# One fused two-layer kernel on one Trainium2 core: the copies that empty a side product's PSUM bank are given out at the head of the next turn instead of behind that turn's exponential and maxima

## The chip, the cores and the metric

The kernel runs on one core of one Trainium2 chip, in one launch. The metric is the device time of that launch in microseconds (us); the time of a kernel is the median over its runs.

## What is computed

The input is x, 16 sequences of 512 tokens with 128 features, in float32. Six residual steps follow each other, each on a layer norm of x:

```
x = x + 0.5 * ffn0(layernorm(x))   # 64 channels, 16 relu hinges each, back to 128
x = x + attn0(layernorm(x))        # 16 query heads of 8, 4 key/value heads, rope, causal softmax
x = x + 0.5 * ffn0(layernorm(x))
x = x + 0.5 * ffn1(layernorm(x))   # 8 experts of 128-512-128, each takes its 128 best tokens
x = x + attn1(layernorm(x))        # a gated linear recurrence over the tokens, 64 channels
x = x + 0.5 * ffn1(layernorm(x))
```

The softmax of `attn0` is over 512 keys for each of 16 x 16 x 512 rows, with the row's maximum subtracted; the expert layer routes by softmax and top-k, gathers tokens, runs gelu between two products, and adds the results back.

## The kernel before, in words

**Stages.** The 16 sequences (index b) go through the first layer one behind the other. A main loop (L1073 to L1102) has one pass per sequence. A pass has 44 turns: 4 groups of heads (r) times 11 banks (`BANKS`, L544). In each turn the generator `weights` (L610) issues for sequence b one bank of transposed scores `ps_st` on TensorE (PE; L622), the exponential that reads it into `pt` on ScalarE (ACT; L625) and the causal mask on GpSimd (POOL; L627). In the same turn `maxima` (L550) issues for sequence b + 1 one bank of scores `ps_sc` (L560, L564) and the row maximum that reads it on VectorE (DVE; L569 for one head, L574 for several). After the 16 passes comes the expert layer twice, with the recurrence between: `experts` (L835) is then the main generator, and again one turn follows another.

**Side work.** Everything else is a set of Python generators in two lists, `urgent` and `sides`. `turn()` (L1046) steps each of them once per turn, behind the main work, and so fills the gaps: the norms and their transposes (`norm` L250, `turned` L285: `kan_x`, then `ps_t`, then `kan_xT`), the first feed-forward (`kan` L299: `kan_s`, eight hinges `kan_h` on ACT at L329, products into `ps_kg`, `ps_ko`), the projections and rope of the attention (`attn_in` L375), the splitting of queries and keys into three bf16 parts on ACT and POOL (`parts` L353), the attention's outputs (`outputs` L633: products into `ps_av`, copy to `oT` L651, transposes into `ps_oq` L656, division into `y` L660 and L661), the output projection (`stage_out` L666), routing (L700), gathering and transposing of tokens (`dispatch` L812), and the recurrence (L981).

**Banks.** A side product takes one of two PSUM buffers (`mm`, `bufs=2`, reached through `bank()`, L222); the scores have two buffers each (`scp`, `stp`, L108 and L109), the outputs `ps_av` and the hinge sums `ps_kg` one each. A PE product that takes a buffer again has to wait until the copy that empties it is done, and a product that reads the copy has to wait for it too.

**Order.** Tensor, Scalar, Vector and GpSimd instructions run in the order in which the program issues them (`manual_schedule`, L185); the order of the DMA issues on SyncE (SP) is left to the framework. A side product is issued in one turn, then its generator yields; the instruction that empties its bank is issued when the generator is stepped again in the next turn. By then `weights` and `maxima` of that next turn have been stepped, so on ACT and DVE it stands behind that turn's exponential or maximum. `need` and `take` (L200, L206) keep a budget of work per engine and turn; `need` yields while a turn's budget is spent, `take` only books.

**Where the steps of the prediction lie.** Copies on ACT: `kan_xT`, `yT`, `rope_a`, `rope_b` (all L292), `kan_s` (L307), the emptying of `ps_kg` (L340), `oT` (L651), half of `xin` (L830). On DVE: rope (L387, L393, L401, L407), `va` (L417), `mr` (L599), the division (L660, L661), sums into x (L349, L675, L1023), `scores` (L695), the other half of `xin`, the scan of the recurrence (L1010).

Of the kernel before, what the change touches and what calls it, by code (L numbers as in the profile page):

```python
# [16 lines left out]
P = 128  # L17
# [27 lines left out]
def tile_macaron(  # L45
# [51 lines left out]
    with ExitStack() as ph:  # L97
# [135 lines left out]

        def together(*gs):

            got, live = [None] * len(gs), list(enumerate(gs))
            while live:
                left = []
                for i, g in live:
                    try:  # L240
                        next(g)
                        left.append((i, g))
                    except StopIteration as end:
                        got[i] = end.value
                live = left
                if live:
                    yield
            return got
# [36 lines left out]
        def turned(src, name, pool):  # L285
            ps = yield from bank([P, NT, P], F32, "ps_t", 0.55)
            for c in range(NT):
                nc.tensor.transpose(ps[:, c, :], src[:, c, :], ident)
            yield
            dst = pool.tile([P, S], F32, name=name)  # L290
            take(act=0.6)
            nc.scalar.copy(dst, ps.rearrange("p c q -> p (c q)"))  # L292
            freed()
            yield
            yield from rest(1)
            yield
            return dst

        def kan(b):  # L299

            _, xT = yield from norm(x[b])
            ps = yield from bank([P, S], F32, "ps_s", 0.9)
            nc.tensor.matmul(ps, lhsT=win.rearrange("d a m -> d (a m)"), rhs=xT, start=True, stop=True)
            yield
            sk = w2p.tile([P, S], F32, name="kan_s")
            take(act=0.6)
            nc.scalar.copy(sk, ps)  # L307
            freed()
            yield
            while kan_held[0]:  # L310
                yield
            kan_held[0] = 1

            pg = kap.tile([P, S], F32, name="ps_kg")
            hs = []
            begin = now[0]
            for t in range(HALF + 1):
                while now[0] < begin + 15 * t // 8:
                    yield
                pair = t % 2 == 0 and t > 0  # L320
                work = {"act": 0.8} if t < HALF else {}
                if pair:
                    work["pe"] = 1.0
                if t == 1:
                    work["pool"] = 1.25
                yield from need(**work)
                if t < HALF:
                    h = hp.tile([P, S], F32, name="kan_h")
                    nc.scalar.activation(h, sk, AF.Relu, bias=rbias[:, t : t + 1], scale=kw1[:, t : t + 1])  # L329
                    hs.append(h)  # L330
                if t == 1:
                    nc.gpsimd.tensor_tensor(x[b], x[b], kcst.unsqueeze(1).to_broadcast([P, NT, D]), ALU.add)
                if pair:
                    for i in range(2):
                        nc.tensor.matmul(pg[i * M : (i + 1) * M, :], lhsT=w2d[:, t - 2 + i, :], rhs=hs[t - 2 + i],  # L335
                                         start=(t == 2), stop=(t == HALF))
                yield
            gT = hp.tile([P, S], F32, name="kan_h")
            take(act=0.6)
            nc.scalar.copy(gT, pg)  # L340
            kan_held[0] = 0
            kans[0] -= 1
            yield
            po = yield from bank([P, NT, D], F32, "ps_ko", 0.9)
            for c in range(NT):
                nc.tensor.matmul(po[:, c, :], lhsT=gT[:, bass.ts(c, P)], rhs=wout, start=True, stop=True)
            yield
            take(dve=0.7)
            nc.vector.tensor_add(x[b], po, x[b])  # L349
            freed()  # L350
            yield
# [23 lines left out]
        def attn_in(b, st):  # L375
# [8 lines left out]
            nc.tensor.matmul(pa, lhsT=wq.rearrange("k h d -> k (h d)"), rhs=xT, start=True, stop=True)  # L384
            yield
            take(dve=0.7)
            nc.vector.tensor_mul(ta, pa, rope[:, 0, :])  # L387
            freed()
            pb = yield from bank([P, S], F32, "ps_pb", 0.9)
            nc.tensor.matmul(pb, lhsT=wqr.rearrange("k h d -> k (h d)"), rhs=xT, start=True, stop=True)  # L390
            yield
            take(dve=0.7)
            nc.vector.tensor_mul(tb, pb, rope[:, 1, :])  # L393
            freed()
            pk = yield from bank([2 * KR, S], F32, "ps_pk", 0.9)
            nc.tensor.matmul(pk, lhsT=wk.rearrange("k w h d -> k (w h d)"), rhs=xT, start=True, stop=True)
            yield
# [3 lines left out]
            nc.vector.tensor_mul(ka, pk[0:KR, :], rope[0:KR, 0, :])  # L401
            pv = yield from bank([P, NT, KR], F32, "ps_v", 0.9)
            for c in range(NT):
                nc.tensor.matmul(pv[:, c, :], lhsT=xT[:, bass.ts(c, P)], rhs=wv, start=True, stop=True)
            yield
            take(dve=0.7)
            nc.vector.tensor_mul(kb, pk[KR : 2 * KR, :], rope[KR : 2 * KR, 1, :])  # L407
# [3 lines left out]
            yield  # L411

            take(dve=0.3)
# [3 lines left out]
            nc.vector.tensor_copy(va[:, :, :, 0:HD], pv.rearrange("p c (r d) -> p c r d", d=HD))  # L417
# [160 lines left out]
        def max_rows(b, half, maxs):  # L578
# [15 lines left out]
            for c in range(NT):  # L594
                nc.tensor.transpose(pm[:, c, :], ms[:, c, :, :].rearrange("p i h -> p (i h)"), identb)
            yield
            mr = w2p.tile([3 * H2, S], BF16, name="mr")
            take(dve=0.4)
            nc.vector.tensor_copy(mr, pm.rearrange("p c q -> p (c q)"))  # L599
# [33 lines left out]
        def outputs(b, st, r):  # L633
# [4 lines left out]
            for c in range(NT):  # L638
                if c == 1:
                    yield  # L640
                if c < 2:
                    yield from need(pe=1.0 if c == 0 else 1.4)
                n = S - c * P
                for g in range(NG):
                    nc.tensor.matmul(po[32 * g : 32 * g + 32, c * P : S], lhsT=va[:, c, r, :],  # L645
                                     rhs=pt[:, g, OFF[c] : OFF[c] + n], start=(c == 0), stop=(c == NT - 1))
                if c in (0, NT - 1):
                    yield
            oT = w2p.tile([P, NT, P], F32, name="oT")
            yield from need(act=0.6)  # L650
            nc.scalar.copy(oT.rearrange("p c q -> p (c q)"), po)  # L651
# [3 lines left out]
            for c in range(NT):  # L655
                nc.tensor.transpose(pq[:, c, :, :].rearrange("p r w -> p (r w)"), oT[:, c, :], ident)  # L656
            yield
            rd = small.tile([P, NT, NG, 1], F32, name="rden")
            take(dve=0.55)
            nc.vector.reciprocal(rd, pq[:, :, :, HD : HD + 1])  # L660
            nc.vector.tensor_mul(y[:, :, r, :, :], pq[:, :, :, 0:HD], rd.to_broadcast([P, NT, NG, HD]))  # L661
# [4 lines left out]
        def stage_out(b, st):  # L666
# [4 lines left out]
            for c in range(NT):  # L671
                nc.tensor.matmul(po[:, c, :], lhsT=yT[:, bass.ts(c, P)], rhs=wo, start=True, stop=True)
            yield
            take(dve=0.7)
            nc.vector.tensor_add(x[b], po, x[b])  # L675
# [10 lines left out]
        def gated(k, b):  # L686
# [4 lines left out]
            for c in range(NT):  # L691
                nc.tensor.matmul(ps[:, c, :], lhsT=xT[:, bass.ts(c, P)], rhs=gateT, start=True, stop=True)
            yield
            take(dve=0.2)
            nc.vector.tensor_copy(scores[b // GB][:, :, b % GB, :], ps)  # L695
# [116 lines left out]
        def dispatch():  # L812
            while taken[0] < NR * B:
                yield
            for i in range(0, len(order), 2):
# [10 lines left out]
                for j in range(2):  # L826
                    nc.tensor.transpose(ps[:, j, :], xgs[i // E % 2][:, i % E + j, :], ident)
                yield
                copy = nc.vector.tensor_copy if i % 4 else nc.scalar.copy
                copy(xins[i // E % 2][:, i % E : i % E + 2, :], ps)  # L830
# [150 lines left out]
        def recurrence(pair):  # L981
# [6 lines left out]
            for a in range(2):  # L988
                nc.tensor.matmul(pf[half[a], :], lhsT=wf, rhs=xTs[a], start=True, stop=True)
            yield  # L990
            fg = w2p.tile([P, S], F32, name="fg", tag="kan_s")
            nc.scalar.activation(fg, pf, AF.Tanh, scale=0.5)
# [5 lines left out]
            nc.tensor.matmul(pl, lhsT=wlam, rhs=fg, start=True, stop=True)  # L998
            yield
            lam = w2p.tile([P, S], F32, name="lam", tag="oT")  # L1000
            nc.scalar.activation(lam, pl, AF.Tanh, bias=lbias, scale=0.25)
# [4 lines left out]
            for a in range(2):  # L1006
                nc.tensor.matmul(pu[half[a], :], lhsT=wb, rhs=xTs[a], start=True, stop=True)
            yield
            s = w2p.tile([P, S], F32, name="s", tag="y")
            nc.vector.tensor_tensor_scan(s, lam, pu, 0.0, ALU.mult, ALU.add)  # L1010
# [3 lines left out]
            def leave(a, b):  # L1014
                po = yield from bank([P, NT, D], F32, "ps_h2")
                for c in range(NT):
# [3 lines left out]
                    if c == 1:  # L1020
                        yield
                yield
                nc.vector.tensor_add(x[b], po, x[b])  # L1023
# [22 lines left out]
        def turn():  # L1046
            urgent[:] = [g for g in urgent if step(g)]
# [13 lines left out]
        for _ in range(8):  # L1061
            step(first)
# [10 lines left out]
        for b in range(-1, B):  # L1073
# [12 lines left out]
            for i in range(TURNS):  # L1086
                step(wts)
# [8 lines left out]
                turn()  # L1096
            step(mxs)
# [10 lines left out]
        while step(main) or sides:  # L1108
# [56 lines left out]
```

## Time and profile before

| what | value |
|---|---|
| median of 3 runs | 1751.41 us (1749.4 to 1756.8) |
| the profiled execution's own time | 1746.91 us |
| its span | 1745.2 us, 35245 instructions |
| PE busy | 1636.9 us (94%) |
| PE weight loads busy | 1111.0 us (64%) |
| DVE busy | 1107.3 us (63%) |
| ACT busy | 996.6 us (57%) |
| POOL busy | 977.6 us (56%) |
| mean granted PE clock | 0.971 |

The profile is of one execution. A line of groups gives the source line, the engine, the operation, what is written and read, the number of instructions, their busy time, the mean duration of one in ns, and the idle time of the engine just before them with what ended it. The start and end of a matmul are partly modelled: a row may say 0.38 us where the next matmul starts 0.22 us later. Busy PE is therefore not PE at its peak, and start-to-start times say more. `PEld` is the loading of the stationary operand, which overlaps the products.

### The profile page before, as it was taken

The numbers are of one execution on the slowest core, as the hardware profiler recorded it, in microseconds if no ns is written. First come the engines' busy times: TensorE is split into PE (matmuls) and PEld (weight loads), VectorE is DVE, ScalarE is ACT, GpSimd is POOL, SyncE is SP. The second block draws the span as 40 slices with busy tenths as digits, with TensorE's granted clock in tenths as the row PEclk, the third lists the DMA queues.
The fourth block names the chain that finished last, engine by engine and source line by source line (L and its number), as shares of the span: only waits on it lengthen the run. The fifth ranks groups of instructions, "written<-read, shape, count | busy, mean of one in ns | idle before, by whom it ended". The sixth has DMA issues, their size and how long they took to land. (4 is left out here: it accounts for less than half of the span.)

```text
span 1745.2 us, 35245 instructions
## 1 busy us (share of the span) xinstructions
PE 1636.9 (94%) x12879; PEld 1111.0 (64%) x12879; DVE 1107.3 (63%) x3604; ACT 996.6 (57%) x2000; POOL 977.6 (56%) x1453
## 2 busy tenths in 40 slices
PE   6788999999999999899899899999999999999997
PEld 2334444444444444444444389899988889989997
DVE  6677767777787788788876137643467444672222
ACT  3445667777777776677667654344443334444443
POOL 2524535545565455455534767567663777647773
PEclk9889999999999999999999899999998999999999
DMA  4211111011110111011122113233322233323342
GB/s 117 76 52 36 44 44 43 28 42 51 54 37 32 42 55 47 16 48 54 35 70 63 31 44 73 51 64 73 62 60 45 55 73 63 66 56 71 68 82 48
DMA packets 101753, 94.77 MB, mean 54 GB/s; under 512 B 11859, under 2 KB 90140, under 8 KB 101340
## 3 DMA queue, kind: packets, MB, share of 16 engines
q1 hardware_dynamic: 74512, 67.45, 12.5%
q0 software_dynamic: 26048, 24.93, 8.8%
q8 instruction: 101, 1.65, 0.4%
q14 instruction: 72, 0.59, 0.1%
q10 hardware_dynamic: 1020, 0.15, 0.0%
HBM read 58.93 MB, written 37.49 MB: 55 GB/s over the span
## 5 line engine op out<-in xcount | busy, mean ns | idle before, releaser
L625 ACT ACTIVATE pt<-ps_st 128x512 f32<-128x512 f32 (+1 forms) x704 | 386.9, 561 | 238.3 <-PE ps_st L622 232.9
L627 POOL TENSOR_SCALAR_AFFINE_SELECT pt<-pt 128x128 f32<-128x128 f32 (+2 forms) x704 | 247.0, 355 | 405.0 <-ACT pt L625 400.4
L569 DVE CUSTOM_DVE_ANT_0 below<-ps_sc,causal 128x512 bf16<-128x512 f32 (+1 forms) x512 | 316.5, 618 | 117.2 <-PE ps_sc L564 103.1
L881 ACT ACTIVATE mo<-ps_h 128x512 f32<-128x512 f32 x256 | 153.1, 598 | 262.2 <-PE ps_h L879 262.0
L805 POOL DMA_INDIRECT xg<-xnd,tokI x256 | 249.9, 976 | 80.5 <-issue 42.8
L879 PE MATMUL ps_h<-xin,mw 128*128 128x128 f32 x2048 | 281.1, 281 | 0.0
L894 PE MATMUL ps_y<-mw,mo 128*128 128x128 f32 x2048 | 274.7, 278 | 0.0
L564 PE MATMUL ps_sc<-kp,qp 72*128 72x512 bf16 (+3 forms) x1024 | 260.7, 307 | 10.6 <-DVE maxs L569 8.0
L622 PE MATMUL ps_st<-qp,kp 99*128 99x512 bf16 (+3 forms) x1024 | 259.8, 307 | 5.7 <-ACT pt L625 4.8
L879 PEld LDWEIGHTS ps_h<-xin,mw 128*128 128x128 f32 x2048 | 252.7, 194 | 6.3 <-issue 3.7
L926 POOL DMA_INDIRECT sum<-ye,tokI x124 | 201.3, 1624 | 97.7 <-ACT ye L897 31.2
L894 PEld LDWEIGHTS ps_y<-mw,mo 128*128 128x128 f32 x2048 | 251.7, 194 | 2.3 <-issue 1.0
L622 PEld LDWEIGHTS <-kp 99*128 99x128 bf16 x1024 | 94.2, 101 | 203.8 <-issue 185.4
L329 ACT ACTIVATE kan_h<-kan_s,rbias,kw 128x512 f32<-128x512 f32 x256 | 206.6, 814 | 7.1 <-PE ps_kg L335 6.9
L574 DVE TENSOR_REDUCE maxs<-ps_sc 128x2 f32<-128x512 f32 (+1 forms) x192 | 130.6, 685 | 70.5 <-PE ps_sc L564 69.3
L335 PE MATMUL ps_kg<-kan_h,w2d 128*64 128x512 f32 x512 | 164.7, 640 | 3.1 <-ACT kan_h L329 3.0
L645 PE MATMUL ps_av<-pt,va 128*32 128x512 f32 (+3 forms) x2048 | 166.8, 444 | 0.0
L564 PEld LDWEIGHTS <-qp 72*128 72x128 bf16 x1024 | 97.5, 100 | 55.6 <-issue 33.9
L900 DVE TENSOR_TENSOR mo<-mo 128x128 bf16<-128x128 f32 x132 | 38.3, 290 | 137.8 <-ACT mo L885 137.6
L912 PE MATMUL acc<-mo 128*128 128x128 bf16 x1584 | 113.0, 220 | 6.0 <-DVE mo L900 5.8
L912 PEld LDWEIGHTS <-mo 128*128 128x128 bf16 x1584 | 99.5, 99 | 23.8 <-issue 22.5
L645 PEld LDWEIGHTS ps_av<-pt,va 128*32 128x32 f32 x2048 | 53.6, 109 | 93.0 <-issue 49.7
(195 smaller groups left out, 2308.8 us busy)
## 6 DMA issues: line engine op xcount, KB each, us to landing
qp<-qs SPq DMA_DIRECT2D x64, 288.0 KB
xnd<-kan_x SPq DMA_DIRECT2D x32, 256.0 KB
sum<-x SPq DMA_DIRECT2D x31, 256.0 KB
qs<-qpart SPq DMA_DIRECT2D x48, 128.0 KB
kp<-ks SPq DMA_DIRECT2D x48, 96.0 KB
x<-in_L_attn_x_dram SPq DMA_DIRECT2D x16, 256.0 KB
mw<-in_L_ffn_w_dram SPq DMA_DIRECT2D x16, 256.0 KB
xg<-xnd,tokI POOLq DMA_INDIRECT x256, 2.5
```

The lines of the kernel that those rows point to most:

```text
L329: nc.scalar.activation(h, sk, AF.Relu, bias=rbias[:, t : t + 1], scale=kw1[:, t : t + 1])
L564: nc.tensor.matmul(v[:, u, 0:n], lhsT=qp[r][0 : 9 * HD, g, bass.ts(c, P)], rhs=kp[0 : 9 * HD, r, 0:n], start=alone, stop=(u == len(gs) - 1 ...
L569: nc.vector.tensor_tensor_reduce(below[:, 0:n], v[:, 0, 0:n], causal[:, S - n : S], 1.0, LOWEST, ALU.add, ALU.max, accum_out=maxs[:, c, h ...
L622: nc.tensor.matmul(v[:, u, 0:n], lhsT=kp[ROWS, r, bass.ts(c, P)], rhs=qp[r][ROWS, g, c * P : S], start=True, stop=True)
L625: nc.scalar.activation(o, v[:, :, 0:n], AF.Exp, scale=HD ** -0.5)
L627: nc.gpsimd.affine_select(out=dg, in_=dg, compare_op=ALU.is_ge, fill=0.0, base=0, pattern=[[0, len(gs)], [1, P]], channel_multiplier=-1)
L645: nc.tensor.matmul(po[32 * g : 32 * g + 32, c * P : S], lhsT=va[:, c, r, :], rhs=pt[:, g, OFF[c] : OFF[c] + n], start=(c == 0), stop=(c == ...
L805: nc.gpsimd.indirect_dma_start(out=xgs[i // E % 2][:, i % E, :], out_offset=None, in_=xnd[b], in_offset=bass.IndirectOffsetOnAxis(ap=tokI[ ...
L879: nc.tensor.matmul(pst[:, f, :], lhsT=mw1[e][:, bass.ts(f, P)], rhs=xins[i // E % 2][:, i % E, :], start=True, stop=True)
L894: nc.tensor.matmul(py, lhsT=hs[u][:, f, :], rhs=mw2[e][:, f, :], start=(f == 0), stop=(f == NF - 1))
L912: nc.tensor.matmul(acc[:, c, :], lhsT=sels[u][:, bass.ts(c, P)], rhs=yes[u][:, w, :], start=(e == 0 and c == 0 and w == 0), stop=(e == las ...
L926: nc.gpsimd.indirect_dma_start(out=sums[k, b], out_offset=bass.IndirectOffsetOnAxis(ap=tokI[g][:, n : n + 1], axis=0), in_=ye[:, b % 2 * ( ...
```

## The change

A list `later` and a function `flush()` are added. Where a side product has been issued, the instruction that empties its bank is no longer issued after the generator's next step but put into `later` at once, before the yield. `flush()` stands at the head of every turn, ahead of `weights` and `maxima` (ahead of `experts` in the second part), and issues what has gathered. So on ACT and DVE these instructions stand ahead of the exponential or maximum of the turn, not behind it. What is booked with `take`, and when a bank counts as free for the next product, stays in its place. In `outputs` the copy of `ps_av` to `oT` had waited for budget (`need`); it now only books (`take`). The two memsets of `va` on POOL are issued a turn earlier, with the product `ps_v`. Left in place are the set-up code, the routing's own copies (L729, L755 to L757) and everything that reads no side product (the hinges L329, the parts L356 and L362, the statistics).

The core of the diff; each of the other places has the same form as one of these:

```diff
+        later = []
+
+        def flush():
+            for emit in later:
+                emit()
+            later.clear()
+
...
             for c in range(NT):
                 nc.tensor.transpose(ps[:, c, :], src[:, c, :], ident)
-            yield
             dst = pool.tile([P, S], F32, name=name)
+            later.append(lambda: nc.scalar.copy(dst, ps.rearrange("p c q -> p (c q)")))
+            yield
             take(act=0.6)
-            nc.scalar.copy(dst, ps.rearrange("p c q -> p (c q)"))
             freed()
...
+                if c == NT - 1:
+                    oT = w2p.tile([P, NT, P], F32, name="oT")
+                    later.append(lambda: nc.scalar.copy(oT.rearrange("p c q -> p (c q)"), po))
                 if c in (0, NT - 1):
                     yield
-            oT = w2p.tile([P, NT, P], F32, name="oT")
-            yield from need(act=0.6)
-            nc.scalar.copy(oT.rearrange("p c q -> p (c q)"), po)
+            take(act=0.6)
...
-            yield
             rd = small.tile([P, NT, NG, 1], F32, name="rden")
+
+            def divide():
+                nc.vector.reciprocal(rd, pq[:, :, :, HD : HD + 1])
+                nc.vector.tensor_mul(y[:, :, r, :, :], pq[:, :, :, 0:HD], rd.to_broadcast([P, NT, NG, HD]))
+
+            later.append(divide)
+            yield
             take(dve=0.55)
-            nc.vector.reciprocal(rd, pq[:, :, :, HD : HD + 1])
-            nc.vector.tensor_mul(y[:, :, r, :, :], pq[:, :, :, 0:HD], rd.to_broadcast([P, NT, NG, HD]))
             freed()
...
         def turn():
+            flush()
             urgent[:] = [g for g in urgent if step(g)]
             sides[:] = [g for g in sides if step(g)]
             refill()
...
             for i in range(TURNS):
+                flush()
                 step(wts)
                 step(mxs)
...
-        while step(main) or sides:
+        working = True
+        while working or sides:
+            flush()
+            working = step(main)
             turn()
```

The same is done to `kan` (`kan_s`, the emptying of `ps_kg`, the sum into x), to `attn_in` (four rope products, `va`), to `max_rows` (`mr`), to `stage_out`, `gated`, `dispatch`, `recurrence` and `leave`.

In the built program the order on PE is the same instruction for instruction. Of 2009 instructions on ACT, 291 stand ahead of at least one that they stood behind; of 3476 on DVE, 364; on POOL the 26 memsets of `va`; and on SP, where the framework orders, some 20 of 445 issues stand one to three places elsewhere.

## The prediction, made blind

> **What bounds the kernel now.** I read the page's busy shares first, then busy time by stretch, then PE's waits within stretches, then the order of time around one wait.
>
> ```profile
> PE 1636.9 (94%) x12879; PEld 1111.0 (64%) x12879; DVE 1107.3 (63%) x3604; ACT 996.6 (57%) x2000; POOL 977.6 (56%) x1453
> ```
>
> PE sets the time; no other engine exceeds 64%. By stretch (width, then busy time of PE, PEld, DVE, ACT, POOL, then PE clock, DMA share, GB/s):
>
> ```profile
> 0.00:150.00 150.00, 113.80 (x498) 48.30 (x502) 102.56 (x295) 67.19 (x109) 54.30 (x96) 0.87 0.24 75
> 150.00:250.00 100.00, 90.56 (x639) 44.66 (x635) 72.17 (x232) 61.95 (x118) 50.17 (x104) 0.93 0.14 45
> 250.00:650.00 400.00, 393.78 (x2836) 193.46 (x2837) 310.41 (x1026) 301.90 (x555) 213.47 (x443) 1.00 0.13 43
> 650.00:955.00 305.00, 282.77 (x2045) 138.07 (x2044) 247.12 (x801) 209.05 (x387) 145.68 (x317) 0.98 0.15 47
> ...
> 1300.00:1400.00 100.00, 93.07 (x724) 80.33 (x724) 67.42 (x227) 34.12 (x83) 55.44 (x54) 0.92 0.24 50
> ```
>
> The steady passes (250 to 650) leave PE 6.2 us idle in 400; 650 to 955, where routing joins DVE, 22.2 in 305. Only PE's idle time is to be had, and only what an emptying ends. PE's waits in 250 to 650 are these two (total, times, longest):
>
> ```profile
> PE ps_s L303 <- ACT kan_xT L292: 5.0, 7, 0.7
> PE ps_o L672 <- ACT yT L292: 1.1, 7, 0.2
> ```
>
> and in 650 to 955 the largest are
>
> ```profile
> PE ps_t L288 <- DVE y L661: 6.7, 4, 2.9
> PE ps_ko L346 <- DVE rope_kb L407: 2.1, 1, 2.1
> PE ps_sc L564 <- DVE maxs L574: 1.7, 4, 0.7
> PE ps_sc L564 <- DVE maxs L569: 1.5, 4, 0.5
> PE ps_m L595 <- DVE rope_kb L407: 1.3, 2, 0.7
> ```
>
> All but the two `maxs` rows end on an emptying that the change moves. How one arises (start, duration):
>
> ```profile
> 507.02 0.33 PE L622 MATMUL ps_st<-qp,kp 99*128 99x384 bf16 x1
> 507.14 0.52 ACT L625 ACTIVATE pt<-ps_st 128x384 f32<-128x384 f32 x1
> 508.08 0.62 ACT L362 CAST kpart<-rope_ka 32x512 bf16<-32x512 f32 x1 [0.42 <-POOL rope_ka L359]
> 508.61 0.57 ACT L292 COPY kan_xT<-ps_t 128x512 f32<-128x512 f32 x1
> 509.08 0.95 ACT L625 ACTIVATE pt<-ps_st 128x384 f32<-128x384 f32 x2
> 509.23 1.12 PE L303 MATMUL ps_s<-kan_xT,win 128*128 128x512 f32 x2 [0.71 <-ACT kan_xT L292]
> ```
>
> The transposes behind this copy ended at 506.86. The copy ran 1.75 us later, behind the turn's exponential and a cast that waited for POOL; PE stood until it ended. The same stall repeats in each pass.
>
> [...] the copy above had its input and still waited for its queue; a 0.38 us score product is followed 0.22 us later by the next. So a PE wait of w on the page is w + 0.16 from start to start, and I add 0.16 us per wait removed. [...] Here some waits are for the bank (`ps_t` for `y`), others for the data (`ps_s` for `kan_xT`); both end with the same copy. [...] after the 2.9 us wait that ended at 909.4, the clock in 909 to 913 is 0.57.
>
> **The change, part by part.** The order on PE is the same, instruction for instruction; ACT, DVE and POOL execute the same instructions. Only the time at which banks and copies, exponentials and maxima are ready can move.
>
> *Removed: waits for emptyings.* An emptying moves ahead of one exponential (0.46 to 0.60 us), or one reduction (0.55 to 0.69), and of the casts or statistics between, and of their own waits. I credit the smaller of the wait and the distance moved.
> 250 to 650: 6.1 us in 14 waits, each of at most 0.7 against 1.1 or more moved: 6.1 + 14 x 0.16 = 8.3.
> 650 to 955: `y` four times 0.65 = 2.6 of its 6.7 (the rest is DVE's backlog ahead of it); `rope_kb` 1.1 of the one long wait and 1.3 of the two short; `va` 1.5, `kan_xT` 1.1, `mr` 0.7, `rope_a` and `rope_b` 1.2, `kan_h` of L340 0.3; with 0.16 for ten or so removed whole, 11.5.
> 150 to 250: of `rope_kb` 2.3, `y` 2.7 and `kan_xT` 0.6, about 5.8 with the 0.16s. 955 to 1050: 2.2 (mostly `oT`). Expert part: `xin` 2.7 and the scan 1.9, of which about 3.7. Before 150: 0.9.
> Sum of credits: 32.4 us.
>
> *Added: exponentials and maxima are later.* Behind an emptying now wait its turn's exponential, and behind that the hinges, casts and POOL's mask. PE waits for the exponential when it takes the same `ps_st` two banks on. I measured this spare time for every bank: start of its first L622 minus end of the exponential two banks before. In 250 to 650 the smallest is 0.145 us, a tenth lie under 0.25, the median is 1.29; 0.05 of each is the signal (509.18 to 509.23 above). Each moved emptying makes its exponential later by its own duration, 0.57 to 0.60, less what ACT idled there; what exceeds the spare time is a new stall. Over the 94 moves in 250 to 650 that is 8.7 us in 28 turns (mostly `oT` and `kan_xT`, in the short turns in the middle of a head group); 3.3 in 650 to 955, 1.5, 0.7 and 1.0 in the other three: 15.2. The same for maxima: 3.6, nearly all before 150 and in 650 to 955. Together 18.8 if nothing absorbs them. In the expert part the gelu and the scaled copies have more spare time than a copy takes; cost zero, up to 2 if not.
>
> *How the two meet.* I walked the stretch 506 to 514 by hand. `oT` ahead puts the exponential of 506.3 back to 506.9 and the L622 of 507.02 to 507.38; `kan_xT` ahead (now 507.3) puts the next L622 from 507.80 to 508.35; L303 starts at 508.9, not 509.23; then two copies stand ahead of the exponential of 511.05, and the L622 of 511.85 is no earlier than before; L672 starts 0.3 earlier. Stalls of 1.19 leave, delays of 1.11 arrive, 0.35 remains. So in the steady passes the credit nearly cancels: seven times 0.35, less 0.2 a pass for delays elsewhere in it, is 1.0. Elsewhere credit less cost is 11.5 - 4.5 = 7.0, 5.8 - 0.7 = 5.1, 2.2 - 1.5 = 0.7, 3.7 in the expert part, and 0.9 - 2.8 = -1.9 at the start. Total 15.6. In the routing stretch DVE has a backlog of two to three instructions when PE waits, so what is next late is often another DVE result; I keep about 70%: **11 us**.
>
> *Moved at no cost.* The memsets of `va` (0.42 and 0.13 us) go ahead of one mask; the mask's readers, the `ps_av` products, come turns later; without that cover 0.55 a pass, 8 us. `take` for `need` in `outputs` changes no budget that matters, since PE's order is unchanged. SP: some 20 issues shift one to three places of about 0.7 us (a part of the keys goes behind the row maxima's transfer); kp and qp are for a later pass; PE's stalls ending on a DMA there are two, 2.9 us, so I bound it by 0 and 3 and take 0. `mr` comes earlier, and its DMA with it.
>
> Base: 1746.9 (profiled execution; span 1745.2) - 11 = 1735.9. Runs stand at 1751.41 / 1746.91 = 1.0026 of it: **1740 us**.
>
> **Rivals.**
> *No change.* Credit is passed on everywhere as in the steady pass (30% of 32.4 = 9.7) and half the costs arrive (9.4): 1751. For it: the walk. Against: outside the steady passes few moved exponentials are short of spare time.
> *Slower: late exponentials.* The costs arrive in full (18.8) and reach the hinges: four `ps_kg` products at 466.80 take 1.64 us and at 481.20 1.95, against 1.01, because they wait for a hinge that stands behind an exponential; a further 0.33 at two places in 16 passes is 10.5. With half the credit (16.2): 29.3 - 16.2 = +13, 1764. It decides once the delays not absorbed exceed the credit kept. Against it: an emptying's input is complete on PE before the turn's scores are, so it never holds ACT for PE longer than the exponential did.
> *Clock.* From the clocks by stretch, half-rate time after 150 is about 60 us (14, 12, 13, 5, 16), some 30 us of loss, each begun by a wait of 2 us or more. If shorter waits spare a third of it, 10 more: 1730. It can also go the other way by a few us[...].
> *Not done as said*: excluded by the order on ACT and DVE.
>
> **Chances.** Forecast 0.52 (its own range 1732 to 1749), no change 0.21, slower 0.13, clock 0.14. Low 1728 leaves about half of the clock case out, high 1756 the slower one; with the tails about 0.2. A measurement can tell 0.5%, 8.8 us, from no change. Faster by more, under 1742.6: two thirds of the forecast and the clock case, 0.48. Slower, over 1760.2: most of that rival, 0.12. Same: 0.40.
>
> **What would show it.** `kan_xT`, `yT` and `oT` start within 0.7 us of their products' end; PE's waits for `kan_xT` at L303 vanish; the waits for `y` drop by about 0.6 each; PE's waits for `pt` at L622 grow by several us. The forecast is wrong if those grow by more than the others shrink, if `ps_kg` pairs lengthen, or if half-rate stretches come or go.

## The result, and the profile after

| | before | after |
|---|---|---|
| median | 1751.39 us (1749.4 to 1756.8, 4 runs) | 1731.26 us (1727.0 to 1734.0, 4 runs) |
| the profiled execution, its span | 1746.9, 1745.2 | 1733.8, 1732.0 |
| its mean granted PE clock | 0.971 | 0.972 |

The ratio is 0.9885, 95% interval [0.9869, 0.9901]: 20.1 us faster by the medians, 13.1 by the two profiled executions. The traces can explain the 13.1 only. Two other runs of the changed kernel took 1727.0 and 1728.7 us at a mean clock of 0.980 and 0.979, so part of the rest is clock that differs from run to run. (The trace's record of the PE clock has two values, 1.0 and 0.5; a half-rate stretch below is a time at 0.5.)

The changed kernel's page, busy shares:

```profile
PE 1629.2 (94%) x12879; PEld 1112.0 (64%) x12879; DVE 1119.1 (65%) x3604; ACT 1001.4 (58%) x2000; POOL 980.0 (57%) x1453
```

PE has 7.7 us less for the same products (the clock has a part in it, see below). DVE has 11.8 us more, with the same 3604 instructions. By stretch, in the columns shown for the kernel before:

```profile
0.00:150.00 150.00, 112.37 (x492) 48.31 (x493) 101.94 (x293) 67.11 (x108) 54.32 (x95) 0.85 0.24 75
150.00:250.00 100.00, 94.07 (x649) 46.35 (x648) 73.76 (x241) 64.60 (x120) 50.93 (x107) 0.91 0.14 47
250.00:650.00 400.00, 392.91 (x2824) 194.62 (x2824) 321.54 (x1017) 299.56 (x551) 213.19 (x440) 1.00 0.13 43
650.00:955.00 305.00, 285.60 (x2129) 141.84 (x2127) 248.57 (x815) 219.76 (x405) 156.29 (x334) 1.00 0.15 49
...
1300.00:1400.00 100.00, 94.45 (x764) 84.31 (x763) 59.14 (x209) 34.73 (x83) 56.15 (x54) 0.91 0.28 56
```

The steady stretch does 12 products fewer than before in the same 400 us, with 11.1 us more on DVE. From 650 to 955 PE does 84 more, at a clock of 1.00 (before 0.98). PE's waits from 250 to 650, then from 650 to 955:

```profile
PE ps_sc L574 <- DVE maxs L584: 3.4, 7, 0.5
PE ps_sc L574 <- DVE maxs L579: 3.4, 14, 0.4
```

```profile
PE ps_t L297 <- DVE y L672: 5.0, 4, 1.9
PE ps_st L632 <- ACT pt L635: 4.1, 10, 0.7
PE ps_kg L344 <- ACT kan_h L338: 2.0, 2, 1.0
PE ps_sc L570 <- DVE maxs L579: 1.8, 4, 0.6
...
PE ps_ko L356 <- DVE rope_kb L415: 0.8, 1, 0.8
```

In the steady stretch the waits for `kan_xT` and `yT` are gone, and 6.8 us of waits for maxima stand in their place. From 650 to 955 the waits for `y` and `rope_kb` have shrunk.

**Where the time went.** PE's order is the same in all kernels of this study, so I compare when PE begins the first score product (L622 before, L632 after) of each pass. After less before, summed up: +0.6 us at pass 1, -1.6 at pass 3, +0.7 at pass 9, -13.1 at pass 15, -14.1 at the first expert product, -13.1 at the end. A steady pass (the median of passes 4 to 8) takes 55.57 us before and 55.97 after: it has become longer. All of the gain lies in passes 1 to 2 and 9 to 15.

**What holds the steady pass.** The groups of DVE in 250 to 650 that make `kan_x`, in the changed kernel:

```profile
L283 DVE TENSOR_SCALAR kan_x<-x,ln_mv,ln_rstd 128x128 f32<-128x128 f32 x28 | 21.3, 801 | 0.0
L287 DVE TENSOR_TENSOR kan_x<-x,ln_rstd 128x512 f32<-128x512 f32 x21 | 15.6, 742 | 0.0
```

and in the kernel before:

```profile
L278 DVE TENSOR_TENSOR kan_x<-x,ln_rstd 128x512 f32<-128x512 f32 x21 | 15.6, 742 | 0.0
L274 DVE TENSOR_SCALAR kan_x<-x,ln_mv,ln_rstd 128x128 f32<-128x128 f32 x28 | 10.5, 419 | 0.0
```

The same 28 instructions (L274, now L283; they normalise x ahead of the router, four per pass) take 801 ns in place of 419: 10.8 us more, in a window in which DVE grew by 11.1 in all (per whole pass, 1.5 of 1.9). The timeline of the changed kernel shows how (start, duration; "x2" and "x3" are instructions in a row):

```profile
506.94 0.56 ACT L299 COPY kan_xT<-ps_t 128x512 f32<-128x512 f32 x1
508.48 1.02 PE L312 MATMUL ps_s<-kan_xT,win 128*128 128x512 f32 x2
...
511.06 1.35 POOL L637 TENSOR_SCALAR_AFFINE_SELECT pt<-pt 128x256 f32<-128x256 f32 x3
511.14 1.61 DVE L283 TENSOR_SCALAR kan_x<-x,ln_mv,ln_rstd 128x128 f32<-128x128 f32 x2
...
512.67 0.68 DVE L584 TENSOR_REDUCE maxs<-ps_sc 128x4 f32<-128x512 f32 x1
...
513.12 1.27 POOL L341 TENSOR_TENSOR x<-x,kcst 128x512 f32<-128x512 f32 x1
513.27 1.46 DVE L283 TENSOR_SCALAR kan_x<-x,ln_mv,ln_rstd 128x128 f32<-128x128 f32 x2
...
513.40 0.38 PE L574 MATMUL ps_sc<-kp,qp 72*128 72x512 bf16 x1 [0.53 <-DVE maxs L584]
```

`kan_xT` starts early and its product has no wait, as meant. But the first `kan_x` of 511.14 starts just after POOL's masks have started, takes 1.35 us by its own record, and is done 0.08 us after the last of the three; the second of the pair takes 0.34. The next pair falls on POOL's addition of 1.27 us and takes 1.20 + 0.33. In the kernel before the two pairs stand like this:

```profile
511.99 0.59 DVE L274 TENSOR_SCALAR kan_x<-x,ln_mv,ln_rstd 128x128 f32<-128x128 f32 x2
513.10 0.91 DVE L274 TENSOR_SCALAR kan_x<-x,ln_mv,ln_rstd 128x128 f32<-128x128 f32 x2
```

Three of these four took 0.34 us, one 0.66. The maximum behind is late by what is lost, and PE waits for its bank. The profile shows DVE as busy in this, not idle (0.0 in the rows above): only the duration of the instruction tells.

What these traces show is this: beside POOL's work the instruction takes 1.35 and 1.20 us where 0.33 is usual, and both times it ends 0.08 us after that work. The first of these lasted over three short masks in a row, not one instruction. How the two engines hold each other up no trace shows; below it is called the collision.

### The profile page after: what moved, and what is told of

It reads as the page before. It is cut to its first block, busy times and chain, and to the rows that moved or that the text cites. A ratio compares the mean times of both kernels' runs of the same rounds, so it can differ in the third digit from the quotient of the medians.

```text
span 1732.0 us, 35235 instructions
## 1 busy us (share of the span) xinstructions
PE 1629.2 (94%) x12879; PEld 1112.0 (64%) x12879; DVE 1119.1 (65%) x3604; ACT 1001.4 (58%) x2000; POOL 980.0 (57%) x1453
## 5 line engine op out<-in xcount | busy, mean ns | idle before, releaser
L635 ACT ACTIVATE pt<-ps_st 128x512 f32<-128x512 f32 (+1 forms) x704 | 379.6, 560 | 130.9 <-PE ps_st L632 127.9
L632 PE MATMUL ps_st<-qp,kp 99*128 99x512 bf16 (+3 forms) x1024 | 258.7, 305 | 9.9 <-ACT pt L635 9.2
L632 PEld LDWEIGHTS <-kp 99*128 99x128 bf16 x1024 | 93.5, 100 | 204.6 <-issue 186.8
```

The source lines that it names most:

```text
L632: nc.tensor.matmul(v[:, u, 0:n], lhsT=kp[ROWS, r, bass.ts(c, P)], rhs=qp[r][ROWS, g, c * P : S], start=True, stop=True)
L635: nc.scalar.activation(o, v[:, :, 0:n], AF.Exp, scale=HD ** -0.5)
```

## Experiments

Each kernel was timed beside the kernel before on its own chip, and ratios are to that. Five chips were used in all; the kernel before took 1785.5 us on that of e1 to e4, 1832.7 with e5 to e8, 1746.8 with e9 to e11 and 1748.4 with e12. In the first eight runs the expert part, here all that follows the last bank of scores, took 785 to 834 us (750 on the first chip), for reasons that I did not settle, so their ratios say little of the passes, and I read these from traces: there the chips agree (the changed kernel's steady pass is 55.97 and 55.99 us on two of them). "Pass" is the steady pass (median). "Up to 9" is what has been lost or won against the profile before when pass 9 begins, "9 to 16" what is lost or won from there to the last bank of scores of pass 15, in us.

| run | early | normalisation `kan_x` | ratio, interval | pass | up to 9 | 9 to 16 |
|---|---|---|---|---|---|---|
| before | none | as before | 1 | 55.57 | | |
| after | all | as before | 0.9885 [0.9869, 0.9901] | 55.97 | +0.7 | -14.9 |
| e1 | ScalarE's | as before | 1.0045 [1.0022, 1.0068] | 56.64 | +3.7 | -0.3 |
| e2 | VectorE's | as before | 0.9898 [0.9870, 0.9927] | 55.59 | -3.6 | -12.7 |
| e3 | ScalarE's; VectorE's from pass 9 | as before | 0.9955 [0.9938, 0.9973] | 56.64 | +8.0 | -8.1 |
| e4 | all | summing form | 0.9879 [0.9851, 0.9908] | 54.49 | -12.3 | -15.7 |
| e5 | all | as before | 0.9801 [0.9761, 0.9840] | 55.99 | +0.1 | -13.9 |
| e6 | none | summing form | 1.0000 [0.9972, 1.0027] | 56.24 | +5.7 | +3.8 |
| e7 | ScalarE's | summing form | 0.9965 [0.9942, 0.9987] | 55.42 | +1.4 | +1.6 |
| e8 | all | summing form, two steps | 1.0001 [0.9976, 1.0025] | 55.79 | -0.4 | +4.3 |
| e9 | none | as before | 1.0042 [1.0028, 1.0057] | 56.24 | +3.2 | -0.4 |
| e10 | all | on ScalarE | 0.9936 [0.9923, 0.9949] | 55.13 | -4.0 | -14.2 |
| e11 | the division | as before | 0.9986 [0.9977, 0.9995] | 55.61 | -1.2 | +0.6 |
| e12 | all | on ScalarE in the passes | 0.9906 [0.9889, 0.9922] | 55.67 | -1.7 | -14.6 |

In e1 to e11 the two memsets of `va` stand where the change puts them. So the order to hold e1, e2, e6, e7 and e11 against in the passes is that of e9, which has the memsets alone (56.24), not that of the kernel before. One rule says what is given out early; the rest is issued behind its `take`, as before:

```diff
+        def give(engine, emit):
+            if early(engine):
+                later.append(emit)
+                return lambda: None
+            return emit
...
-            later.append(lambda: nc.scalar.copy(sk, ps))
+            put = give("act", lambda: nc.scalar.copy(sk, ps))
             yield
             take(act=0.6)
+            put()
```

**One half of the change each.** My first theory was that the copies moved on ScalarE win in the steady passes and the operations moved on VectorE lose there. e1 has `early` true for "act", e2 for "dve", e3 for "act" and, from pass 9 on, for "dve" too.

> Only the emptyings on ScalarE stand ahead of the exponential; those on VectorE stand behind the maxima as before. Theory D (the gain comes from VectorE's emptyings in the passes with routing, the loss in the steady passes from maxima that now come late): a steady pass takes 55.0 us instead of 55.6 before and 56.0 changed, passes 10 to 15 gain only 3 of the 14 us, in all 8 us faster (0.995). Rival A (the gain is ScalarE's, whose copies are the ones that PE waited for in every pass): nearly the whole 20 us stays (0.989), passes 10 to 15 included.

> Only the emptyings on VectorE stand ahead of the maxima; those on ScalarE stand behind the exponential as before. Theory D: a steady pass takes 56.0 us or more, passes 10 to 15 gain 9 us or more, in all 8 to 10 us faster (0.995). Rival A: steady pass as before, 55.6, passes 10 to 15 gain at most 4, in all 4 us or less (0.998).

> ScalarE's emptyings go ahead everywhere, VectorE's only from pass 9 on, where routing begins to load VectorE. Theory D: a steady pass takes 55.0 us, passes 10 to 15 gain what the full change gains, in all 5 to 6 us faster than the full change, 24 us faster than before (0.986). Rival A: no different from the full change (0.989). If the passes before 3 need VectorE's emptyings, 2 to 3 us of it are lost.

The theory fell. ScalarE's half alone makes the pass longer (56.64 us) and the kernel slower; VectorE's half alone leaves the pass at the length that it has in the kernel before, 0.65 us below e9, and brings nearly all of the gain (in the passes 16.3 us, where the whole change brings 14.2). e3 had been meant as a better version and wins less than half as much. The `kan_x` of e1 that normalises ahead of the router (L283 in the changed kernel), in 250 to 650:

```profile
L294 DVE TENSOR_SCALAR kan_x<-x,ln_mv,ln_rstd 128x128 f32<-128x128 f32 x28 | 19.4, 734 | 0.0
```

and both kinds in e2:

```profile
L298 DVE TENSOR_TENSOR kan_x<-x,ln_rstd 128x512 f32<-128x512 f32 x21 | 20.8, 990 | 0.0
L294 DVE TENSOR_SCALAR kan_x<-x,ln_mv,ln_rstd 128x128 f32<-128x128 f32 x28 | 11.5, 451 | 0.0
```

In e1 the `kan_x` ahead of the router takes 734 ns where e9, without ScalarE's half, has 418. I take it that this half shifts exponentials, and so masks, onto it. In e2 it is the other kind that has grown, by 5.2 us in the stretch; DVE is busy 2.0 us more per pass than before, and yet the pass is no longer. What this costs and what the early operations save come out even there; I did not separate them.

**The collision taken away.** That the form of the normalisation that also sums would not be held up was an assumption of mine; e4 is the whole change with it:

```diff
                     nc.vector.tensor_scalar(xl[:, c, :], xt[:, c, :], mv[:, c, 0:1], rstd[:, c : c + 1],
-                                            ALU.subtract, ALU.mult)
+                                            ALU.subtract, ALU.mult, accum_out=unused[:, c : c + 1])
```

In this form the kernel leaves out the multiplication by the inverse deviation (so in e6 and e7 too). The router and the experts then work on other values, so of these three only the passes are read.

> The full change, but the normalization that writes kan_x (TENSOR_SCALAR, 128x128, the one whose mean went from 0.42 to 0.80 us in the steady passes) also writes out an unused accumulator. Theory P (it got slower because it now falls onto GpSimd's masks[...]): its duration in the steady passes is the same everywhere, under 0.5 us with the accumulator's read, a steady pass is back at 55.5 us or below, 3 us faster than the full change (0.987). Rival M (maxima are late simply because an emptying stands ahead of each): the pass stays at 56.0 and the time at 0.989 or a little more.

The pass falls to 54.49 us, the shortest of all; from pass 3 to 9 the trace lists no wait of PE at all. The form's mean is 398 ns here, 400 in e6 and 399 in e7: one duration in three orders. Its groups in e4, in 250 to 650:

```profile
L295 DVE TENSOR_SCALAR_CACHE_REDUCE kan_x<-x,ln_mv,ln_rstd 128x128 f32<-128x128 f32 x28 | 10.1, 398 | 0.0
L295 DVE DVE_READ_ACCUMULATOR kan_x<-x,ln_mv,ln_rstd 128x1 f32 x28 | 2.3, 81 | 0.0
```

**Form or collision?** The next four ran on one chip. e5 is the change itself again. e6 and e7 put the form of e4 into the order before and into e1. e8 is the whole change in two operations of that form, the second multiplying, with nothing left out:

```diff
-                    nc.vector.tensor_scalar(xl[:, c, :], xt[:, c, :], mv[:, c, 0:1], rstd[:, c : c + 1],
-                                            ALU.subtract, ALU.mult)
+                    nc.vector.tensor_scalar(xl[:, c, :], xt[:, c, :], mv[:, c, 0:1], None,
+                                            ALU.subtract, ALU.add, accum_out=unused[:, c : c + 1])
+                    nc.vector.tensor_scalar(xl[:, c, :], xl[:, c, :], rstd[:, c : c + 1], None,
+                                            ALU.mult, ALU.add, accum_out=unused[:, c : c + 1])
```

> The whole change once more, on the chip that ran the half changes, whose own kernel before takes 1785.5 us. If the two halves simply add: the exponential half alone was 1.0045 and the VectorE half alone 0.9898, so 0.9942. If the VectorE half does in the whole change what it does alone, and the ScalarE half costs nothing beside it: 0.990. The first chip showed 0.9885. Steady pass: 56.0 us as on the first chip (before 55.6).

> The order of the kernel before, with only the four normalising subtractions per pass in the form that also sums (the multiplication by the inverse deviation is left out there, and stays out of the output). If the collision of this operation with GpSimd's masks is something that the change brought about, little is to be had here: kan_x falls from 419 ns to about 320 ns with its sum, four per pass, beside PE's work: 0 to 0.3 us a pass, ratio 0.997 to 1.000. If the form itself is what gave the earlier full change without the collision its 1.1 us a pass, it gives the same here: steady pass 54.4, ratio about 0.989.

> Only ScalarE's emptyings early, and the normalising subtraction in the form that sums (the multiplication by the inverse deviation is left out). If ScalarE's half lengthens the steady pass through the collision (56.6 us against 55.6), the pass falls under that of the kernel before, to 54.5 to 55.3, and the ratio to 0.985 to 0.995. If it lengthens it through the exponentials and copies behind which other ScalarE work waits, the pass stays at 56.3 to 56.6 and the ratio at 1.003.

> The whole change, with the normalisation in two operations of the form that sums, one subtracting and one multiplying, so that the output is the reference's. VectorE has some 0.64 us for each of the four instead of 0.80 as the collision left them, in about 2.6 us per pass and without variation. If the collision is what lengthens the pass, it is 54.5 to 55.0 us and the ratio 0.982 to 0.989, better than the change as it is. If VectorE's busy time is what counts, the pass stays at 56 us and the ratio at that of the whole change.

e5 repeats the passes of the change, 13.8 us by the last; its ratio is lower than this gives, which must come from outside the passes; the kernel before has no profile on that chip, and it stays open. In e6 the form wins nothing over e9, which has the same order (both 56.24), so the form is not a gain in itself. In e7 ScalarE's half, which had lengthened the pass, lies below the kernel before (55.42) and 0.82 below e6: the lengthening was the collision, not late exponentials. e8 shows no collision (means of 340 and 347 ns in 250 to 650), but its two operations keep DVE busy for 0.66 us per normalisation, not much less than the collision had (0.76), and its pass is again near that of the change. So it is DVE's time at this place that counts, whether the collision or a longer form takes it.

Pairs of runs that differ only in this normalisation say how much. From pass 3 to 9, with time in which two records overlap counted once, the pass grows by 1.48 us for 1.62 more of `kan_x` per pass (after against e4), 1.22 for 1.20 (e1, e7), 1.30 for 1.24 (e8, e4), and not at all for none (e6, e9): about one for one. DVE is busy 80% of the steady stretch and yet paces it, through the maxima queued on it. This holds within one order, not across orders, as e2 shows, and only as long as the maxima are what PE waits for: e10, without this work on DVE, stays 0.64 above e4, with PE waiting for `pt`.

That e8 lost all gain from pass 9 to 16 I had not expected. Its half-rate time there is 34 us, against 3 to 7 in e4, e5 and the change. Half of PE's busy time in such a stretch, where the recorded clock is 0.5, is an estimate of what it costs (a stretch of 10.2 us in e3, below, cost 4.6): 16.3 us in e8, 3.1 in e5, so 13 of the 18 us between them.

**The memsets, the engine, and the division.** e9 has the order before on PE, ACT and DVE, and only the memsets moved. e10 takes the normalisation to ScalarE:

```diff
+                nc.gpsimd.tensor_tensor(shift, mv[:, :, 0], rstd, ALU.mult)
+                nc.gpsimd.tensor_scalar(shift, shift, -1.0, None, ALU.mult)
...
-                    nc.vector.tensor_scalar(xl[:, c, :], xt[:, c, :], mv[:, c, 0:1], rstd[:, c : c + 1],
-                                            ALU.subtract, ALU.mult)
+                    nc.scalar.activation(xl[:, c, :], xt[:, c, :], AF.Identity, bias=shift[:, c : c + 1],
+                                         scale=rstd[:, c : c + 1])
```

e11 has only `divide` early (L671, L672).

> The order of the kernel before on PE, VectorE, ScalarE and SyncE; of the change only what it moves on GpSimd's queue and in the code, the two memsets of va, is left in. I had put this at nothing. Passes within 0.3 us of those of the kernel before in sum, ratio 0.998 to 1.002. If the memsets' place matters, some of the gain before pass 9 is here.

> The whole change, with the normalisation of one kind of pass moved to ScalarE as four activations with scale and bias (GpSimd works out the bias in two small operations), [...] the output stays the reference's. If what lengthens the steady pass and the passes 10 to 15 is VectorE's maxima coming late, by the collision or by its busy time: steady pass 54.2 to 54.9 us (56.0 with the change), passes 9 to 16 at least 15 us shorter in all than before, ratio 0.972 to 0.985, better than the whole change by 8 to 13 us. If ScalarE has no room for four more operations of about 0.3 us a pass, the pass stays above 55.5.

> Only the two operations that make y out of a turned product (a reciprocal and a multiplication, 16 pairs per pass) are given out ahead; all other emptyings are where they were before. VectorE's half alone won 12.7 us in passes 9 to 16, 3.6 before pass 9. If PE's waits for y are what that was, nearly all of the 12.7 is here: 10 to 13 us, ratio 0.990 to 0.994. If the gain is from the rotary products, va and the additions to x, it is below 4 us.

e9 missed: the memsets that I had put at nothing lengthen the pass by 0.67 us and the kernel by 0.4%. They fill a time in which POOL stood idle (0.97 us ahead of the mask at 501.42 in the kernel before), and its additions behind them come 0.5 to 0.8 us earlier in the pass. The first of these now meets a small cast on DVE, which takes 1.02 us there in place of 0.26. The next meets the other `kan_x`, a product of two SBUF operands, which the cast has made 0.7 us later. Each happens once per pass. The casts of e9 in 250 to 650, then those of the kernel before:

```profile
L619 DVE CAST ms<-ms_r 128x32 bf16<-128x32 f32 x15 | 8.6, 570 | 0.0
```

```profile
L589 DVE CAST ms<-ms_r 128x32 bf16<-128x32 f32 x15 | 3.2, 214 | 0.0
```

The product in e9's timeline, and its group in 250 to 650 (742 ns before):

```profile
505.04 1.25 POOL L453 TENSOR_TENSOR rope_ka<-rope_ka,rope_kb 32x512 f32<-32x512 f32 x1
...
505.64 1.29 DVE L298 TENSOR_TENSOR kan_x<-x,ln_rstd 128x512 f32<-128x512 f32 x1
...
506.26 0.82 POOL L658 TENSOR_SCALAR_AFFINE_SELECT pt<-pt 128x128 f32<-128x128 f32 x1
```

```profile
L298 DVE TENSOR_TENSOR kan_x<-x,ln_rstd 128x512 f32<-128x512 f32 x21 | 19.0, 906 | 0.0
```

The product ends 0.64 us after the addition, about its time alone (0.68), and the mask that starts at 506.26 takes 0.82 us where one of its size takes 0.29 with nothing beside it (0.75 beside this product in the kernel before): as if each stood for the other in turn. Cast and product together take 1.25 us more per pass, of which 0.67 reach its length. e2, e6 and e11, which share the memsets' place, show both (casts of 572 to 626 ns).

e10 shortened the pass to 55.13, less than expected (PE's waits in it are now for `pt`, 2.5 us in six passes), and its expert part took 758.1 us in place of 750.6: there ScalarE's activation of `kan_x` stands among the gelus (from 980 to 1560, 136 of 482 ns each, where the changed kernel has 136 of 360 ns on DVE).

e11 missed too. The division alone gives all that VectorE's half gave in the steady pass (55.61, against 56.24 in e9), but nothing in passes 9 to 16. What differs there between e11 and e2 is therefore the rest of that half. PE's waits in passes 9 to 15, in e11:

```profile
PE ps_t L308 <- DVE y L694: 5.2, 4, 2.3
...
PE ps_ko L370 <- DVE rope_kb L433: 2.1, 1, 2.1
...
PE ps_m L625 <- DVE rope_kb L433: 1.3, 2, 0.7
...
PE ps_t L308 <- DVE va L444: 1.0, 1, 1.0
...
PE ps_oq L689 <- DVE mr L627: 0.7, 1, 0.7
PE ps_t L308 <- DVE rope_b L417: 0.7, 1, 0.7
PE ps_pk L423 <- DVE rope_a L410: 0.6, 1, 0.6
PE ps_s L324 <- DVE va L444: 0.5, 1, 0.5
```

and in e2:

```profile
PE ps_t L308 <- DVE y L694: 5.2, 4, 1.9
PE ps_st L653 <- ACT pt L656: 3.7, 8, 1.0
PE ps_t L308 <- DVE kan_x L298: 2.5, 1, 2.5
```

with no row left for the rope products, `va` and `mr`: 6.9 us of waits gone, and 5.5 by the whole lists, since some others grew. The trace's clock gives the rest: the half-rate time in these passes is 23.9 us in e11 and 6.8 in e2, and half of PE's busy time in it is 11.1 and 2.7, so by this estimate about 8.4 us less was lost.

That the clock alone can do this is seen in e3. Its pass 13 and that of the changed kernel have the same list of waits, to the tenth. The stretch of this pass, in e3:

```profile
843.90:901.50 57.60, 53.02 (x361) 25.08 (x359) 44.75 (x139) 35.57 (x66) 25.57 (x58) 0.91 0.15 52
```

and in the changed kernel:

```profile
835.30:888.30 53.00, 48.42 (x361) 23.77 (x359) 44.49 (x139) 35.41 (x66) 26.24 (x58) 1.00 0.17 56
```

The same 361 products took 4.6 us more at a clock of 0.91, through one half-rate stretch of 10.2 us.

With the estimated loss of the clock taken off, the time from pass 9 to 16 sorts the runs. It is 369.3 us in the changed kernel and 369.6 in e3, 367.1 to 370.2 in all runs with VectorE's half early there except e8 (373.7), and 374.7 to 378.9 in those without, the kernel before (376.7) and e11 (375.2) among them. So VectorE's half shortens these passes without the clock too. Its half-rate time is mostly lower as well, 3 to 10 us against 17 to 31, but 17 in e3 and 34 in e8: shorter waits and less half-rate time go together in most runs; that the one brings the other is not shown.

**A last version.** e12 is e10 with ScalarE's normalisation only in the passes, and the memsets where the kernel before has them.

```diff
+            scaled = whole and at[0] < B
...
             yield
             take(dve=0.3)
+            nc.gpsimd.memset(va[:, :, :, HD:32], 0.0)
+            nc.gpsimd.memset(va[:, :, :, HD : HD + 1], 1.0)
```

> The whole change with the normalisation on ScalarE as before, but only in the passes; in the expert part, where ScalarE's Gelu is in the way, it goes back to VectorE. And va's two memsets stand again where the kernel before has them. The memsets alone had cost 0.66 us a pass in the old order, by holding up the normalising multiplication of the other kind, which takes 0.74 us unharmed; in the whole change and with the normalisation on ScalarE it already takes 0.74 to 0.75. So, if they cost only by that collision, their place is worth nothing here: steady pass 55.0 to 55.3 as in the last version (55.13), passes over by 18 us before the kernel before; if they cost by their own 0.54 us on GpSimd, 54.5 to 54.8. The expert part takes 749 to 752 us, as in the kernel before and with the change (749.6 and 750.6), where it took 758.1 with the normalisation on ScalarE; in all a ratio of 0.988 to 0.990 on a chip where the expert part is as on the first.

The expert part is back (748.7 us), and the span is 1728.1, 3.9 us below that of the change. But the memsets' old place, better in the old order, is worse in this one: the product that is L287 in the changed kernel is held up again (924 ns), and the pass is 55.67 in place of 55.13. I had expected no effect. The ratio of 0.9906 [0.9889, 0.9922] cannot be told from that of the change. e10's passes with e12's expert part would have been the combination to run; it was not run.

## Why the prediction came out as it did

The sign and the range were right: 1731.3 against 1740 within 1728 to 1756. The mechanism was right for the passes with routing, though about half of what came there is clock; for the steady passes it was wrong. By its own steps, profiled execution against profiled execution:

| stretch | predicted, before the 70% | measured |
|---|---|---|
| start | +1.9 | +0.6 (up to pass 1) |
| 150 to 250 | -5.1 | -2.2 (passes 1 and 2) |
| 250 to 650 | -1.0 | +2.3 (passes 3 to 8) |
| 650 to 955 | -7.0 | -13.8 (passes 9 to 14) |
| 955 to 1050 | -0.7 | -1.0 (pass 15 to the first expert product) |
| expert part | -3.7 | +1.0 |
| sum | -15.6, kept -11 | -13.1 |

The sum came near by errors of both signs, which is luck: passes 1 to 8 and the expert part gave less than forecast, the stretch with routing twice as much.

- *Removed waits.* As predicted: the waits for `kan_xT` and `yT` are gone; `rope_kb` in 650 to 955 fell from 3.4 to 0.8 (credited 2.4); `va`, `mr`, `rope_a` and `rope_b` are gone. `y` fell by 1.7 of 6.7, not 2.6. In 250 to 955 all 46 copies to `kan_xT` start within 0.6 us of the end of their products and all 52 to `oT` within 0.3; of 13 to `yT`, 11 start within 0.1 us and two more than 2 us late.
- *Late exponentials, 8.7 us in 250 to 650.* Too high: PE began 28 banks right behind an exponential, as many as forecast, but stood at most 0.2 us at each, some 3 us in all from start to start. In 650 to 955 the price of 3.3 was right: the waits for `pt` rose from 1.0 to 4.1. The groups of four at `ps_kg` did not become long more often (15 long ones against 16 in 250 to 650, 7 against 7 in 650 to 955), though the two longest went from 2.4 and 2.7 to 3.2 us; the slower rival found little ground.
- *Late maxima, 0.6 in 250 to 650* (what its sums leave of the 3.6). This is the step that failed: PE's waits for maxima there are 6.8 us. I had priced an emptying ahead of a maximum by its own duration and held all other DVE durations fixed. They are not: the shift of masks onto `kan_x` cost 1.5 us per pass (after against e4).
- *The walk of 506 to 514, 0.15 us a pass in the end.* Too low. Without the collision e4's pass is 1.08 us shorter than before. In the whole change a gain of this size and a loss of 1.5 cancel to +0.4.
- *Moved at no cost: the memsets.* Wrong: their cover was taken to be the mask's readers, and these indeed had time. But the 0.54 us move the later POOL instructions against DVE. It cost 0.67 us a pass in the old order (e9), and the old place cost 0.54 in e12's. What it is worth inside the change alone was not tried.
- *650 to 955 and the clock rival.* The mechanism of the forecast and that of the rival came together. From pass 9 to 16, 14.9 us went. The half-rate time there fell from 20.5 to 3.4 us, and its estimated cost from 9.0 to 1.5 us: about 7.5 us is clock, about 7.4 shorter waits. The shorter waits came with VectorE's rope, `va` and `mr` (e2 against e11), which my credit had as 5.8 us without the clock. That half-rate stretches went was among my own signs that the forecast is wrong. And the rival had each of them begun by a wait of 2 us or more; the one at 871.9 in the kernel before follows gaps of 0.7 at most. It went the other way too: before pass 9 the half-rate time rose from 51.2 to 61.4 us, which is why the mean clock is the same.
- *Expert part.* The 3.7 us did not arrive. By the last expert product PE was 1.0 us further ahead than at the first, and 2.0 were lost behind it; why was not tried.
- *Profiled execution to median.* I multiplied by 1.0026; the profiled run of the changed kernel lies above its median, not below, and 7 of the 9 us between forecast and result are this.

In the two kernels the half-rate stretches, but for the last of a run, are multiples of 3.4 us long, from 3.4 to 20.5. What begins one is not shown. Those in passes 9 to 15 of the kernel before stand at waits of 3.0 us at most. In e3 the 10 us before the stretch at 873.8 have gaps of PE of 0.7 us at most, which the changed kernel has there too, each to 0.01 us, without going to half rate.

## What to carry to other kernels

After a change of order, compare the mean duration of each group on every engine, of the untouched ones above all: an instruction that has become longer with the same operands can be a wait that no list of waits shows (here 419 to 801 ns, with 0.0 us of idle time). Where VectorE and GpSimd both work from SBUF, as here, a step moved past something on either queue need not be free: the memsets cost 0.67 us a pass in e9. Look where the pairs meet in a pass and price both. And split a gain by stage and by clock before crediting it to a mechanism: here a quarter of a per cent came and went with half-rate stretches in a single pass.

## What was not expected of the hardware

- Normalising 128x128 on DVE took 0.33 us alone and up to 1.36 behind POOL's masks; four of them per pass were enough to turn a gain of about 1.1 us into a loss of 0.4. A product of two SBUF operands took 0.68 us at its shortest and 1.29 beside POOL's addition (e9), and the POOL mask behind it 0.82 in place of 0.29. A cast of 128x32 took 1.02 us beside such an addition in place of 0.26 (e9).
- A steady pass repeats to within 0.03 us of its median in nearly all passes, and the median from chip to chip to 0.02 (55.97, 55.99), so differences of 0.1 us a pass can be read from one profile where whole times scatter by 0.3% and more.
- An engine that is busy 80% set the pace of one that is busy 98%: in three pairs of runs that differ in one operation alone, each us more of it on DVE lengthened the pass by 0.9 to 1.05 us.
- PE went to half rate for 10.2 us though the 10 us before had gaps of 0.7 us at most, and in another run with the same order and the same gaps it did not; that alone was 4.6 us.
